# A graph network in one kernel: the middle stages in a written order, lin in operands 500 nodes wide, the edges' steps by twos

## The chip, the cores and the metric

The kernel runs on one core of a Trainium2 chip. The core has five engines that work at the same time and wait for each other through semaphores: TensorE (PE, with its weight loads as PEld), VectorE (DVE), ScalarE (ACT), GpSimd (POOL), and SyncE (SP), which issues most of the DMAs. The metric is the device time of one execution in microseconds (us); lower is better. All times below are in us unless marked otherwise.

## The reference

The input is x (1250 nodes x 1024), 20,000 directed edges with weights, and the parameters of two layers, each behind a layer norm and a ReLU, each added to its input. Cut to what matters:

```python
def layer0(x, src, dst, weight, wenc, benc, wdec, bdec, conv, lin):
    h = sigmoid(x @ wenc.T + benc)                   # 1250 x 500
    h2 = h @ conv
    agg = segment_sum(h2[src] * weight[:, None], dst)
    return (agg + h @ lin.T) @ wdec.T + bdec         # 1250 x 1024

def layer1(x, src, dst, W, b):                       # self loops added
    h = x @ W.T + b
    deg = count(row) + 1                             # row = src, or the node itself
    norm = deg[row] ** -0.5 * deg[col] ** -0.5
    return segment_sum(norm[:, None] * h[col], row)

h = relu(layernorm(x)); x = x + layer0(h, ...)
h = relu(layernorm(x)); x = x + layer1(h, ...)
```

## The kernel before

**Numbers in halves.** A float32 product is made of three matmuls on operands split into a high part (rounded for PE) and a low part (the rest): high x high, high x low, low x high. `product` (L342 to L352) issues them; its matmul stands at L347, so the encoder, lin, conv, the aggregation and the decoder all show that line, and are told apart by the tiles' names (penc, plin, pconv, pagg, pdec). A split costs a copy on ACT (high part) and a subtraction on DVE or POOL (low part).

**Stages.** Nodes are handled in 10 tiles of T = 125, or in NCH = 5 chunks of CH = 250. In the order of time:

- *Encoder* (`encode`): layer norm, transposition, x @ wenc.T and the sigmoid per chunk. It writes hT, the hidden values transposed (500 features as EC = 4 blocks of 125 rows, nodes as columns) in a high and a low part. Beside it the edges are read and turned into key columns for the one-hots.
- *lin* (`linear`): per chunk four products of 3 x 4 matmuls of 250 columns (plin). ACT copies each to hl.
- *conv* (`convolve`): per node tile one product of 12 matmuls of 500 columns (pconv), split into h2.
- *Aggregation* (`aggregate`): the edges become a dense matrix A (weights by source and destination), made while conv and the aggregation run. Per chunk four products of 3 x 10 matmuls of 250 columns (pagg). Each is closed by three operations: DVE adds it to hl (L702), ACT copies the high part (L703), DVE subtracts for the low part (L704). The results, agg, are the decoder's operands.
- *Decoder* (`decode`): per tile two halves of 12 matmuls of 512 columns (pdec), added to x by DVE; the sums go to DRAM through SP and are normed for the second layer.
- *Second layer*: products pz (L952) on counts of edges, the counts being loaded back transposed from DRAM (c_d to cr, L799), then pout (L1175), scaled by dinv, and the output.

**The edges' steps.** A step is PB = 5 groups of 5 destination nodes; there are 50. `one_hots` makes the operands of a step on DVE with three operations: L482 (640 elements per partition, which source residue), L486 (250, which block and destination), L490 (750, the same times the weight's three parts). `adjacency` takes a step that has been built: 15 small matmuls on PE (poh, 128 x 100 and 128 x 50), copies by ACT of the weights' high parts into A (L523, three pieces by APARTS) and of the counts (L529), and the low parts by DVE (L534, three pieces). After every fifth step a node tile's counts are whole: DVE adds the diagonal (L536), reduces the counts for the degrees (L537), and SP stores them to c_d (L538). `edge_work(n)`, called after each product or within it, adds n to an account, and while a whole step is owed, builds one and consumes one; two built steps stay ahead.

**Order of the work.** The encoder and everything from the decoder on stand in a written order (`tc.manual_schedule()`): each engine runs its instructions as the program has them. From lin to the decoder a planner reorders them (the context is left after the encoder and entered again before the decoder); it took 54 of lin's matmuls ahead of the encoder's last 8. Three pools of PSUM give the buffers: ps_acc with four accumulators for the products, ps_t with two, ps_oh with two for the steps' poh. Places in SBUF come from an arena whose offsets are a written list, PLAN, one for each allocation in order of the program; an instruction that writes a place waits for the last users of what lay there.

**Behind the aggregation.** `load` and `split` bring wdec in (four pieces, low parts on POOL at L632) after chunk 3's aggregation. The degrees' partial sums, degp, are summed by DVE, raised to the power -1/2 by POOL (dinv, L777), and stored by SP (L778). After this store in SP's order come the decoder's transposing loads of the counts (L799), the loads of x (L196) and the stores of the sums (x_d).

The calls of the stages, before:

```python
in_order.close()
for c in range(NCH):
    linear(c, lin, lambda: edge_work(0.8))
    if c == 1:
        cv = split_square("conv")
for c in range(NCH):
    convolve(c, cv, lambda: edge_work(1))
for c in range(NCH):
    aggregate(c, lambda: edge_work(0.8))
```

Of the kernel before, what the change touches and what calls it, by code (L numbers as in the profile page):

```python
# [35 lines left out]
P = 128  # L36
# [40 lines left out]
class Arena:  # L77
# [33 lines left out]
    6272, 1500, 3354, 1375, 0, 599, 1087, 3162, 3857, 346, 2032, 3729, 5890, 1750, 3479, 5390,  # L111
    4227, 4887, 2574, 4637, 5137, 5640, 2000, 3447, 1718, 1215, 5900, 6150, 2265, 567, 2824,
    3322, 4081, 535, 4509, 1718, 663, 2973, 1250, 2515, 0, 3857, 3953, 4951, 4919, 282, 32, 5140,
    1000, 1660, 1500, 398, 3223, 282, 494, 1718, 750, 526, 6118, 2015, 5890, 2829, 423, 5079,
    4111, 4008, 1250, 1500, 4638, 3399, 4606, 4866, 3777, 2831, 647, 5000, 3296, 5515, 5412,
    5309, 1853, 5103, 4263, 500, 4513, 3081, 4763, 3432, 2956, 5229, 3638, 4013, 3888, 5435,
    4866, 3329, 3081, 3535, 5332, 5140, 5060, 397, 4763, 0, 3535, 1750, 2000, 6297, 3208, 5265,
    5140, 103, 6015, 2162, 0, 5640, 2314, 3458, 250, 2497, 2417, 2721, 2064, 6297, 2618, 1147,
    147, 500, 750, 1016, 2337, 2721, 5037, 2456, 6265, 1141, 4410, 147, 44, 2314, 4660, 1141,
    1622, 2706, 3458, 4263, 3598, 1292, 6265, 5060, 3848, 5515, 147, 4638, 4079, 1542, 3862, 0,  # L120
    2328, 3348, 4182, 147, 3990, 5343, 4246, 4502, 3206, 5093, 0, 3598, 1672, 1280, 6178, 2956,
    5013, 6265, 5810, 5890, 6098, 5679, 4758, 5599, 2956, 2064, 5970, 4886, 5807, 4998, 6258,
    4758, 2496, 5679, 6112, 4838, 5952, 6240, 3428, 4758, 3348, 5639, 5879, 3990, 5839, 5599,
    5359, 5559, 2456, 5015, 4303, 5759, 4855, 5719, 5679, 5199, 6160, 5919, 6240, 3518, 6080,
    5519, 2888, 4695, 3348, 5359, 5759, 5039, 2888, 5519, 4879, 5199, 6240, 6200, 6160, 4695,
    3508, 5279, 5799, 5960, 5639, 3702, 5879, 6000, 3350, 5359, 3622, 3862, 5960, 5239, 6240,
    3478, 4695, 5079, 4855, 4951, 2916, 5519, 5639, 3734, 5799, 5159, 3606, 6000, 5279, 5385,
    1800, 6240, 1672, 1928, 2888, 5599, 5079, 4695, 5257, 5513, 3271, 4823, 2456, 5960, 2592,
    5671, 3143, 1280, 1536, 1408, 2135, 5921, 6022, 2928, 3007, 2513, 4445, 6150, 2849, 6229,
    4366, 2056, 6308, 5129, 5592, 2263, 2842, 6150, 4317, 5943, 5671, 2921, 2513, 6272, 2056,  # L130
    2592, 2135, 3064, 4445, 2842, 6022, 4616, 5592, 5079, 5943, 2263, 2056, 2985, 4303, 3064,
    5693, 6321, 4616, 2857, 5614, 2592, 2513, 4488,
# [4 lines left out]
def kernel(  # L137
# [35 lines left out]
    APARTS = ((0, 4), (4, 4), (8, 2))  # L173
# [301 lines left out]
    def one_hots(n):  # L475

        gs = slice(n * PB, (n + 1) * PB)
        eb, ek, ew = edges["eb"], edges["ek"], edges["ew"]
        t = arena.tile([P, PB * (P + 4 * M)], BF16, f"oh{n}")
        bo = t[:, : PB * P].rearrange("p (g b) -> p g b", g=PB)  # L480
        mv = t[:, PB * P :].rearrange("p (g q m) -> p g q m", g=PB, q=4)
        nc.vector.tensor_tensor(  # L482
            pairs(bo), pairs(cols).unsqueeze(1).to_broadcast([P, PB, P // 2, 2]),
            eb[:, gs].unsqueeze(2).to_broadcast([P, PB, P // 2, 2]), op=OP.is_equal,
        )
        nc.vector.tensor_tensor(  # L486
            pairs(mv[:, :, 0, :]), pairs(cols[:, :M]).unsqueeze(1).to_broadcast([P, PB, M // 2, 2]),
            ek[:, gs].unsqueeze(2).to_broadcast([P, PB, M // 2, 2]), op=OP.is_equal,
        )
        nc.vector.tensor_tensor(  # L490
            pairs(mv[:, :, 1:4, :]),
            pairs(mv[:, :, 0, :]).unsqueeze(2).to_broadcast([P, PB, 3, M // 2, 2]),
            ew[:, gs].unsqueeze(3).to_broadcast([P, PB, 3, M // 2, 2]), op=OP.mult,
        )
        built.append((n, bo, mv))

    def adjacency():
# [16 lines left out]
        arena.give(f"oh{n}")  # L514
# [20 lines left out]
        if k == per - 1:  # L535
            nc.vector.tensor_add(C[j][:T, j, :T], C[j][:T, j, :T], ident_b[:T, :T])  # L536
            nc.vector.tensor_reduce(degp[:, :, j], C[j][:T, :, :T], AX.X, OP.add)  # L537
            nc.sync.dma_start(c_d[j], C[j].rearrange("p a d -> p (a d)"))  # L538
            arena.give(f"cnt{j}")

    todo = list(range(NG // PB))
    owed = [0.0]

    def edge_work(n):

        owed[0] += n
        while owed[0] >= 1 - 1e-6 and (todo or built):
            owed[0] -= 1
            if todo:
                one_hots(todo.pop(0))  # L550
            if len(built) > 2 or not todo:
                adjacency()
# [13 lines left out]
    def encode(c, between):  # L566
        hi, lo = hn[c]
        hT[c] = arena.tile([T, 2, EC, CH], FR, f"hT{c}")
# [80 lines left out]
    def linear(c, lin, between):  # L649
        hl[c] = arena.tile([T, EC, CH], F32, f"hl{c}")  # L650
        for ec in range(EC):
            es = slice(ec * T, (ec + 1) * T)
            p = ps_acc.tile([P, 512], F32, tag="acc", name="plin")
            product(
                p[:T, :CH],
                [
                    ([lin(k, s)[:, es] for s in range(2)], [hT[c][:, s, k, :] for s in range(2)])
                    for k in range(EC)
                ],
            )  # L660
            nc.scalar.copy(hl[c][:, ec, :], p[:T, :CH])
            between()

    def convolve(c, cv, between):
        h2[c] = arena.tile([T, 2, 2, EMB], FR, f"h2_{c}")
        for i in range(2):
            p = ps_acc.tile([P, 512], F32, tag="acc", name="pconv")
            ns = slice(i * T, (i + 1) * T)
            product(
                p[:T, :EMB],  # L670
                [
                    ([hT[c][:, s, k, ns] for s in range(2)], [cv(k, s) for s in range(2)])
                    for k in range(EC)
                ],
            )
            nc.scalar.copy(h2[c][:, 0, i, :], p[:T, :EMB])
            nc.vector.tensor_sub(h2[c][:, 1, i, :], p[:T, :EMB], h2[c][:, 0, i, :])
            between()
        arena.give(f"hT{c}")
# [3 lines left out]
    def aggregate(c, between):  # L683
# [23 lines left out]
        arena.give(f"hl{c}")  # L707
# [36 lines left out]
    in_order.close()  # L744
# [3 lines left out]
    for c in range(NCH):  # L748
        linear(c, lin, lambda: edge_work(0.8))
        if c == 1:  # L750
            cv = split_square("conv")
    arena.give("lin0", "lin1")
    for c in range(NCH):
        convolve(c, cv, lambda: edge_work(1))
# [4 lines left out]
    wdec = []  # L759
    for c in range(NCH):  # L760
        aggregate(c, lambda: edge_work(0.8))
# [7 lines left out]
        elif c == 3:  # L769
            wdec.extend(split(f"wdec{k}", nc.gpsimd) for k in range(EC))  # L770
            load_x(1)
    arena.give(*(f"h2_{c}" for c in range(NCH)))
# [6 lines left out]

    in_order.enter_context(tc.manual_schedule())  # L780
# [853 lines left out]
```

## Time and profile before

| | |
|---|---|
| median of 3 runs | 487.01 (486.67 to 487.57) |
| the profiled execution | 487.37, its span 485.6 |
| TensorE's clock granted, mean | 0.993 of full speed |
| busy share of the span | PE 98%, PEld 89%, DVE 69%, ACT 36%, POOL 17% |
| lin | 76.8 to 112.8 |
| conv | 112.8 to 145.1 |
| aggregation | 145.1 to 230.8 |
| decoder | 230.8 to 286.4 |
| second layer, pz and pout | 286.4 to 480 |

The profile is one execution, recorded by the hardware; its span goes from the first recorded instruction to the last one's end, and 1.77 us of the execution's own time lie outside it. The page's first part gives each engine's busy time and its share of the span, with the number of instructions. A table by stage gives the same within chosen windows. The order in time of one engine lists start, length, engine, line, operation, tiles, shape, and, after an x, how many instructions in a row were merged into the row; the length of a merged row runs from the first start to the last end. Matmuls overlap in the pipeline, so a single length (0.28 at 250 columns) is longer than the distance between two starts. The chain that ended last runs through DVE from about 283.5 to 314.4, and from there through PE's pz and pout to the end.

### The profile page before, as it was taken

The numbers are of one execution on the slowest core, as the hardware profiler recorded it, in microseconds if no ns is written. First come the engines' busy times: TensorE is split into PE (matmuls) and PEld (weight loads), VectorE is DVE, ScalarE is ACT, GpSimd is POOL, SyncE is SP. The second block draws the span as 40 slices with busy tenths as digits, with TensorE's granted clock in tenths as the row PEclk, the third lists the DMA queues.
The fourth block names the chain that finished last, engine by engine and source line by source line (L and its number), as shares of the span: only waits on it lengthen the run. The fifth ranks groups of instructions, "written<-read, shape, count | busy, mean of one in ns | idle before, by whom it ended". The sixth has DMA issues, their size and how long they took to land. (4 is left out here: it accounts for less than half of the span.)

```text
span 485.6 us, 9225 instructions
## 1 busy us (share of the span) xinstructions
PE 474.9 (98%) x3614; PEld 431.2 (89%) x3614; DVE 336.0 (69%) x763; ACT 174.3 (36%) x453; POOL 81.5 (17%) x134
## 2 busy tenths in 40 slices
PE   6999999999999999999999999999999999999995
PEld 3999999998889999999878889999998887788784
DVE  6777479977697958884457776968798554555541
ACT  4585543553433243451253345323265021110000
POOL 4734252410000010161123641000000000000000
PEclk9899999999999999999999999999999999999998
DMA  8993103000000204401999621022429064445441
GB/s 284 368 272 85 32 2 84 1 29 28 29 29 28 70 4 135 164 1 29 205 253 262 200 86 45 2 82 92 163 79 236 11 165 112 112 122 128 124 97 49
DMA packets 50899, 52.20 MB, mean 108 GB/s; under 512 B 29728, under 2 KB 39592, under 8 KB 50847
## 3 DMA queue, kind: packets, MB, share of 16 engines
q1 hardware_dynamic: 50449, 51.09, 37.2%
q8 instruction: 30, 0.49, 0.4%
q0 software_dynamic: 320, 0.39, 0.3%
q14 instruction: 22, 0.18, 0.1%
q10 hardware_dynamic: 78, 0.05, 0.0%
HBM read 34.61 MB, written 17.45 MB: 107 GB/s over the span
## 5 line engine op out<-in xcount | busy, mean ns | idle before, releaser
L1175 PE MATMUL pout<-w,zs 128*125 128x512 f32 (+1 forms) x336 | 100.8, 383 | 0.0
L347 PE MATMUL pagg<-A,h 125*125 125x250 f32 x600 | 74.7, 282 | 0.0
L1175 PEld LDWEIGHTS pout<-w,zs 128*125 128x125 f32 x336 | 61.3, 186 | 14.1
L347 PEld LDWEIGHTS pagg<-A,h 125*125 125x125 f32 x600 | 71.4, 187 | 0.1
L347 PE MATMUL pdec<-wdec,agg 126*125 126x512 f32 x240 | 56.2, 395 | 0.0
L347 PEld LDWEIGHTS pdec<-wdec,agg 126*125 126x125 f32 x240 | 44.7, 187 | 11.1
L1183 DVE SCALAR_TENSOR_TENSOR res<-pout,dinv,res 125x512 f32<-125x512 f32 (+1 forms) x21 | 15.2, 725 | 49.5 <-PE pout L1175 49.5
L952 PE MATMUL pz<-cts,y 125*128 125x312 f32 (+1 forms) x320 | 47.3, 307 | 0.2 <-DVE cts L818 0.2
L952 PEld LDWEIGHTS pz<-cts,y 125*128 125x128 f32 x320 | 46.4, 189 | 0.5 <-DVE cts L818 0.5
L523 ACT CAST A<-poh 125x100 fp32r<-125x100 f32 x150 | 25.5, 258 | 49.3 <-PE poh L513 49.3
L534 DVE TENSOR_TENSOR A<-poh,A 125x100 fp32r<-125x100 f32 x150 | 26.9, 234 | 13.3 <-ACT cnt L529 12.8
L952 PE MATMUL pz<-ct,y 125*128 125x312 f32 (+1 forms) x240 | 35.7, 307 | 0.0
L952 PEld LDWEIGHTS pz<-ct,y 125*128 125x128 f32 x240 | 35.0, 189 | 0.1
L347 PE MATMUL penc<-hnh,wenc 128*125 128x250 f32 x256 | 34.3, 283 | 0.0
L482 DVE TENSOR_TENSOR oh<-cols,eb 128x640 bf16<-128x640 bf16 x50 | 25.9, 522 | 8.5 <-PE poh L513 6.2
L347 PEld LDWEIGHTS penc<-hnh,wenc 128*125 128x125 f32 x256 | 31.3, 187 | 0.0
L347 PE MATMUL plin<-hT,lin 125*125 125x250 f32 x240 | 30.1, 282 | 0.0
L347 PEld LDWEIGHTS plin<-hT,lin 125*125 125x125 f32 x240 | 28.6, 187 | 0.0
L347 PE MATMUL pconv<-conv,hT 125*125 125x500 f32 x120 | 28.6, 392 | 0.0
L508 PE MATMUL poh<-oh 128*128 128x100 bf16 x250 | 28.1, 206 | 0.0
L512 PE MATMUL poh<-oh 128*128 128x50 bf16 x250 | 27.1, 187 | 0.0
L513 PE MATMUL poh<-oh 128*128 128x50 bf16 x250 | 27.0, 184 | 0.0
(180 smaller groups left out, 843.4 us busy)
## 6 DMA issues: line engine op xcount, KB each, us to landing
x<-in_x_dram SPq DMA_DIRECT2D x14, 512.0 KB
x_d<-x SPq DMA_DIRECT2D x9, 512.0 KB
res<-x_d SPq DMA_DIRECT2D x9, 512.0 KB
out_dram<-res SPq DMA_DIRECT2D x19, 224.0 KB
c_d<-cnt SPq DMA_DIRECT2D x10, 320.0 KB
cr<-c_d SPq DMA_DIRECT2D x10, 312.5 KB
x<-in_x_dram SPq DMA_DIRECT2D x8, 256.0 KB
wencf<-in_wencT_dram SPq DMA_DIRECT2D x4, 500.0 KB
```

The lines of the kernel that those rows point to most:

```text
L347: nc.tensor.matmul(p, left[i], right[j], start=(part == 0 and n == 0), stop=(part == 2 and n == len(terms) - 1),)
L482: nc.vector.tensor_tensor(pairs(bo), pairs(cols).unsqueeze(1).to_broadcast([P, PB, P // 2, 2]), eb[:, gs].unsqueeze(2).to_broadcast([P, PB ...
L508: nc.tensor.matmul(p[:, g, :], left, mv[:, g, 0:2, :].rearrange("p q m -> p (q m)"), start=True, stop=False,)
L512: nc.tensor.matmul(p[:, g, M:], left, mv[:, g, 2, :], start=False, stop=False)
L513: nc.tensor.matmul(p[:, g, M:], left, mv[:, g, 3, :], start=False, stop=True)
L523: nc.scalar.copy(hi, whole)
L534: nc.vector.tensor_sub(lo, whole, hi)
L952: nc.tensor.matmul(p, left[m, which][:, s, j, :], right[:, j, c0:c1], start=(first and j == 0 and s == 0), stop=(last and j == NP - 1 and ...
L1175: nc.tensor.matmul(acc[u][:T, : cs.stop - cs.start], zs[t][:, i, half, m, :], w1[k][j][:, cs], start=(m == 0 and half == 0 and n == 0), st ...
L1183: nc.vector.scalar_tensor_tensor(x1[t][:, cs], acc[u][:T, : cs.stop - cs.start], dinv[:, t : t + 1], x1[t][:, cs], op0=OP.mult, op1=OP.add,)
```

## The change

Six things are edited.

- The written order is kept from the encoder's end to the decoder: `in_order.close()` and the later entry are removed. What was reordered by the planner now runs as the program has it.
- hT and hl are allocated for two chunks at once (the fifth alone), and `linear` handles such a pair: its products are 500 columns wide for the pairs and 250 for the last chunk. hT and hl are given back by pairs.
- `one_hots` builds two steps (OB = 10 groups) with each of its three operations. `edge_work` acts when two steps are owed: with six steps built, or none left to build, it first consumes two, then builds two. The amounts owed change: 0.8 for each chunk in lin's pairs, 1.2 in conv, 1 at each of the two calls in a product of the aggregation.
- A is one tile per chunk (APARTS of one piece), so L523 and L534 are one operation of 250 elements per step in place of three.
- The counts' diagonal is added by POOL. The degrees' reductions leave `adjacency`: `degrees` does them two at a time at the last ten calls of `beside` (the function called in the aggregation), and the rest, if any, after it. A count's buffer is given back there.
- conv's split stands after lin's first pair (before: after its second chunk), wdec's four splits at four of the same last calls (before: after chunk 3).

The list PLAN is new, as the allocations differ.

```diff
--- before.py
+++ after.py
@@ -108,28 +108,26 @@
 
 
 PLAN = (
...
 )
 
 
@@ -170,7 +168,8 @@
     NW = (E - WIN) // GRAN + 1
     NS = E // GRAN
     PB = 5
-    APARTS = ((0, 4), (4, 4), (8, 2))
+    APARTS = ((0, NT),)
+    OB = 2 * PB
 
     BASE = -(-nc.sbuf_base // 32) * 32
     ctx.enter_context(nc.sbuf_tensor("slab", [P, ARENA // 4], F32))
@@ -474,25 +473,27 @@
 
     def one_hots(n):
 
-        gs = slice(n * PB, (n + 1) * PB)
+        gs = slice(n * OB, (n + 1) * OB)
         eb, ek, ew = edges["eb"], edges["ek"], edges["ew"]
-        t = arena.tile([P, PB * (P + 4 * M)], BF16, f"oh{n}")
-        bo = t[:, : PB * P].rearrange("p (g b) -> p g b", g=PB)
-        mv = t[:, PB * P :].rearrange("p (g q m) -> p g q m", g=PB, q=4)
+        t = arena.tile([P, OB * (P + 4 * M)], BF16, f"oh{n}")
+        bo = t[:, : OB * P].rearrange("p (g b) -> p g b", g=OB)
+        mv = t[:, OB * P :].rearrange("p (g q m) -> p g q m", g=OB, q=4)
         nc.vector.tensor_tensor(
-            pairs(bo), pairs(cols).unsqueeze(1).to_broadcast([P, PB, P // 2, 2]),
-            eb[:, gs].unsqueeze(2).to_broadcast([P, PB, P // 2, 2]), op=OP.is_equal,
+            pairs(bo), pairs(cols).unsqueeze(1).to_broadcast([P, OB, P // 2, 2]),
+            eb[:, gs].unsqueeze(2).to_broadcast([P, OB, P // 2, 2]), op=OP.is_equal,
         )
         nc.vector.tensor_tensor(
-            pairs(mv[:, :, 0, :]), pairs(cols[:, :M]).unsqueeze(1).to_broadcast([P, PB, M // 2, 2]),
-            ek[:, gs].unsqueeze(2).to_broadcast([P, PB, M // 2, 2]), op=OP.is_equal,
+            pairs(mv[:, :, 0, :]), pairs(cols[:, :M]).unsqueeze(1).to_broadcast([P, OB, M // 2, 2]),
+            ek[:, gs].unsqueeze(2).to_broadcast([P, OB, M // 2, 2]), op=OP.is_equal,
         )
         nc.vector.tensor_tensor(
             pairs(mv[:, :, 1:4, :]),
-            pairs(mv[:, :, 0, :]).unsqueeze(2).to_broadcast([P, PB, 3, M // 2, 2]),
-            ew[:, gs].unsqueeze(3).to_broadcast([P, PB, 3, M // 2, 2]), op=OP.mult,
+            pairs(mv[:, :, 0, :]).unsqueeze(2).to_broadcast([P, OB, 3, M // 2, 2]),
+            ew[:, gs].unsqueeze(3).to_broadcast([P, OB, 3, M // 2, 2]), op=OP.mult,
         )
-        built.append((n, bo, mv))
+        for i in range(OB // PB):
+            of = slice(i * PB, (i + 1) * PB)
+            built.append((n * (OB // PB) + i, bo[:, of], mv[:, of]))
 
     def adjacency():
 
@@ -511,7 +512,8 @@
             )
             nc.tensor.matmul(p[:, g, M:], left, mv[:, g, 2, :], start=False, stop=False)
             nc.tensor.matmul(p[:, g, M:], left, mv[:, g, 3, :], start=False, stop=True)
-        arena.give(f"oh{n}")
+        if n % (OB // PB) == OB // PB - 1:
+            arena.give(f"oh{n // (OB // PB)}")
         v = p.rearrange("p g (w a d) -> p w a g d", w=2, d=GS)
         at = slice(i * PB * GS, (i + 1) * PB * GS)
         parts = [
@@ -533,23 +535,33 @@
         for whole, hi, lo in parts:
             nc.vector.tensor_sub(lo, whole, hi)
         if k == per - 1:
-            nc.vector.tensor_add(C[j][:T, j, :T], C[j][:T, j, :T], ident_b[:T, :T])
-            nc.vector.tensor_reduce(degp[:, :, j], C[j][:T, :, :T], AX.X, OP.add)
+            nc.gpsimd.tensor_add(C[j][:T, j, :T], C[j][:T, j, :T], ident_b[:T, :T])
             nc.sync.dma_start(c_d[j], C[j].rearrange("p a d -> p (a d)"))
-            arena.give(f"cnt{j}")
-
-    todo = list(range(NG // PB))
+            counted.append(j)
+
+    counted = []
+
+    def degrees(n):
+
+        for _ in range(n):
+            if counted:
+                j = counted.pop(0)
+                nc.vector.tensor_reduce(degp[:, :, j], C[j][:T, :, :T], AX.X, OP.add)
+                arena.give(f"cnt{j}")
+
+    todo = list(range(NG // OB))
     owed = [0.0]
 
     def edge_work(n):
 
         owed[0] += n
-        while owed[0] >= 1 - 1e-6 and (todo or built):
-            owed[0] -= 1
+        while owed[0] >= 2 - 1e-6 and (todo or built):
+            owed[0] -= 2
+            if len(built) >= 6 or not todo:
+                for _ in range(2):
+                    adjacency()
             if todo:
                 one_hots(todo.pop(0))
-            if len(built) > 2 or not todo:
-                adjacency()
 
 
     hT = {}
@@ -565,7 +577,12 @@
 
     def encode(c, between):
         hi, lo = hn[c]
-        hT[c] = arena.tile([T, 2, EC, CH], FR, f"hT{c}")
+        if c % 2 == 0:
+            wide = min(2, NCH - c) * CH
+            pair = arena.tile([T, 2, EC, wide], FR, f"hT{c}")
+            hT["pair", c] = pair
+            for i in range(wide // CH):
+                hT[c + i] = pair[:, :, :, i * CH : (i + 1) * CH]
 
         def left(k, ec, s):
             return wenc[k // 2][:, s, k % 2, ec * T : (ec + 1) * T]
@@ -647,18 +664,23 @@
     h2 = {}
 
     def linear(c, lin, between):
-        hl[c] = arena.tile([T, EC, CH], F32, f"hl{c}")
+
+        h = hT["pair", c]
+        wide = h.shape[3]
+        pair = arena.tile([T, EC, wide], F32, f"hl{c}")
+        for i in range(wide // CH):
+            hl[c + i] = pair[:, :, i * CH : (i + 1) * CH]
         for ec in range(EC):
             es = slice(ec * T, (ec + 1) * T)
             p = ps_acc.tile([P, 512], F32, tag="acc", name="plin")
             product(
-                p[:T, :CH],
+                p[:T, :wide],
                 [
-                    ([lin(k, s)[:, es] for s in range(2)], [hT[c][:, s, k, :] for s in range(2)])
+                    ([lin(k, s)[:, es] for s in range(2)], [h[:, s, k, :] for s in range(2)])
                     for k in range(EC)
                 ],
             )
-            nc.scalar.copy(hl[c][:, ec, :], p[:T, :CH])
+            nc.scalar.copy(pair[:, ec, :], p[:T, :wide])
             between()
 
     def convolve(c, cv, between):
@@ -676,7 +698,8 @@
             nc.scalar.copy(h2[c][:, 0, i, :], p[:T, :EMB])
             nc.vector.tensor_sub(h2[c][:, 1, i, :], p[:T, :EMB], h2[c][:, 0, i, :])
             between()
-        arena.give(f"hT{c}")
+        if c % 2 == 1 or c == NCH - 1:
+            arena.give(f"hT{c - c % 2}")
 
     aggT = {}
 
@@ -704,7 +727,8 @@
             nc.vector.tensor_sub(agg[:T, 1, ec], h, agg[:T, 0, ec])
             between()
         arena.give(*(f"A{c}_{i}" for i in range(len(APARTS))))
-        arena.give(f"hl{c}")
+        if c % 2 == 1 or c == NCH - 1:
+            arena.give(f"hl{c - c % 2}")
 
 
     parts = {}
@@ -741,24 +765,36 @@
         if c + 1 < NCH:
             begin_chunk(c + 1)
         encode(c, lambda n: between((c, n)))
-    in_order.close()
     cv = None
     lin = parts["lin"]
     arena.give(*(f"wenc{j}" for j in range(KD // 2)))
-    for c in range(NCH):
-        linear(c, lin, lambda: edge_work(0.8))
-        if c == 1:
+    for c in range(0, NCH, 2):
+        wide = hT["pair", c].shape[3] // CH
+        linear(c, lin, lambda: edge_work(0.8 * wide))
+        if c == 0:
             cv = split_square("conv")
     arena.give("lin0", "lin1")
     for c in range(NCH):
-        convolve(c, cv, lambda: edge_work(1))
+        convolve(c, cv, lambda: edge_work(1.2))
     arena.give("conv0", "conv1")
 
 
     wdec_v = wdecT.rearrange("(k p) e -> p k e", p=T)
     wdec = []
+
+    beside_left = [2 * EC * NCH]
+
+    def beside():
+        edge_work(1)
+        beside_left[0] -= 1
+        n = 2 * EC + 2 - beside_left[0]
+        if n > 0:
+            degrees(2)
+            if n <= EC:
+                wdec.append(split(f"wdec{n - 1}", nc.gpsimd))
+
     for c in range(NCH):
-        aggregate(c, lambda: edge_work(0.8))
+        aggregate(c, beside)
         if c == 1:
             load(T, wdec_v[:, 0, :], "wdec0", bdec)
             load(T, wdec_v[:, 1, :], "wdec1")
@@ -767,8 +803,8 @@
             load(T, wdec_v[:, 3, :], "wdec3")
             load_x(0)
         elif c == 3:
-            wdec.extend(split(f"wdec{k}", nc.gpsimd) for k in range(EC))
             load_x(1)
+    degrees(NT)
     arena.give(*(f"h2_{c}" for c in range(NCH)))
     arena.give("ed4")
     dinv = const.tile([T, NT], F32, name="dinv")
@@ -776,8 +812,6 @@
     nc.vector.tensor_reduce(deg, degp, AX.X, OP.add)
     nc.gpsimd.tensor_tensor(dinv, deg, half_neg[:T], op=OP.pow)
     nc.sync.dma_start(dinv_d.rearrange("(t p) -> p t", p=T), dinv)
-
-    in_order.enter_context(tc.manual_schedule())
```

## The prediction

> **What bounds the kernel now.** I read the page's busy shares first, then the engines' busy time by stage, then the order in time of TensorE (PE), of the DMA queue SP and of VectorE (DVE). Page and stages (columns of the second: window, its length, busy time and count for PE, PEld, DVE, ACT, POOL, then clock, DMA share, GB/s):
>
> ```profile
> PE 474.9 (98%) x3614; PEld 431.2 (89%) x3614; DVE 336.0 (69%) x763; ACT 174.3 (36%) x453; POOL 81.5 (17%) x134
> ...
> 76.80:112.80 36.00, 36.00 (x434) 35.56 (x433) 30.05 (x95) 17.70 (x71) 6.61 (x6) 1.00 0.15 47
> 112.80:145.10 32.30, 32.30 (x271) 26.51 (x270) 26.02 (x80) 12.04 (x49) 0.15 (x1) 1.00 0.06 22
> 145.10:213.90 68.80, 68.80 (x868) 68.05 (x867) 54.86 (x183) 28.77 (x131) 8.22 (x17) 1.00 0.21 71
> 213.90:230.80 16.90, 16.90 (x156) 16.86 (x156) 8.50 (x15) 3.46 (x10) 7.01 (x5) 1.00 0.10 21
> 230.80:286.40 55.60, 55.60 (x240) 44.50 (x240) 35.88 (x57) 21.38 (x27) 19.05 (x41) 1.00 0.85 215
> ```
>
> These are lin, conv, the aggregation with edges, its end, and the decoder. PE has no idle time in any of them, at full clock; no other engine is full. So what the change takes from DVE and ACT is worth nothing by itself: only PE's own work counts, and any new wait of PE. How closely PE is packed, from its order in time (start, length, merged matmuls):
>
> ```profile
> 97.03 3.49 PE L347 MATMUL plin<-hT,lin 125*125 125x250 f32 x28
> ...
> 101.35 5.26 PE L347 MATMUL plin<-hT,lin 125*125 125x250 f32 x43
> ...
> 118.06 5.89 PE L347 MATMUL pconv<-conv,hT 125*125 125x500 f32 x25
> ```
>
> A run lasts from its first start to its last end. Less the last matmul's own length (0.28 at 250 columns, 0.39 at 500) and the 0.08 us by which the first interval after a group of edge matmuls is longer (0.197 instead of 0.117 between single starts), the pitch is (5.26-0.28-0.08)/42 = 0.1167 us at 250 columns and (5.89-0.39-0.08)/24 = 0.2258 at 500.
>
> **The change, part by part.**
>
> *lin 500 wide.* 192 of the 240 matmuls of 250 columns become 96 of 500; the last chunk keeps 48. 192 x 0.1167 - 96 x 0.2258 = 22.41 - 21.68 = 0.73 us less, on PE's path. The Trainium skill, "TensorE: Matmul & The Clock Gate", section "Wait — 56ns, not 53.3ns?", has warm matmuls start N/2.4 GHz plus about 2.5 ns apart: 0.1067 and 0.2108, so 96 x 2.5 ns = 0.24 us saved. The rows lie above both figures (0.1167, 0.2258) and decide: 0.7, with 0.24 as the low end. ACT's copies become ten of 500 and four of 250 in place of twenty; nothing waits for them within a stage.
>
> *Edges by twos.* On PE the edge work is 50 steps of 15 matmuls. In the order of time they now stand in 31 groups, 12 of one step (0.50 us) and 19 of two (0.987). Each group costs 0.08 at the re-entry. By twos there are 25: six merges of two groups, each 2 x (0.50+0.08) - (0.987+0.08) = 0.09, together 0.56 us less, on the path.
>
> On DVE, single starts in a row give pitches of 0.20, 0.40 and 0.46 us for the one-hots' 250, 640 and 750 elements (L486, L482, L490): 0.07 + 0.52 ns per element. Two steps cost 2 x 1.06 = 2.12; ten groups at once 0.33+0.74+0.85 = 1.92. Splitting A's low part (L534) goes from three operations (0.46) to one of 250 (0.32, L702's pitch at that size). A pair of steps thus costs 2.56 on DVE. In the aggregation one pair falls to each product of 30 matmuls: PE 30 x 0.1167 + 1.07 = 4.57; DVE 2.56 + add, wait for ACT and subtract of agg (1.3) = 3.9. ACT: four copies of 250 (0.42, L529's row) and one of agg (0.40) = 2.1. The edge pair's PSUM banks come free when ACT has copied both parts and DVE has subtracted, some 1.4 and 2.2 us after the pair begins; the next pair comes 4.57 later. Three pairs of one-hots are ahead. No wait of PE: zero.
>
> *Counts' diagonal to POOL, conv and wdec splits beside it.* The add (L536, 0.216 on DVE) goes to POOL, for which I estimate 0.4 to 1 (its bf16 or fp32 operations of 125x256 take 0.46 to 0.73): ten times, off the path, only the store of the count waits. A rule of the Trainium skill speaks against this, in "SBUF — State Buffer", section "Who interferes with whom": DVE operations with two SBUF inputs and POOL operations that read SBUF exclude each other for the whole instruction, while a tensor_reduce never contends. The trace agrees (DVE's and POOL's order in time):
>
> ```profile
> 73.57 3.58 DVE L482 TENSOR_TENSOR oh<-cols,eb 128x640 bf16<-128x640 bf16 x4
> ...
> 73.26 2.33 POOL L632 TENSOR_TENSOR lin<-lin1f,lin 125x1000 fp32r<-125x1000 f32 x1
> ```
>
> The first of these four one-hots took 2.38 instead of 0.48. Where this bites after the change: conv's two splits, issued together after the first lin pair, are 2 x 2.34 of POOL (before: 3.69 at 85.9 and 2.34 at 95.8, ten us apart). Serialised with two sets of one-hots (1.92 each) that makes about 8.5 us of DVE, whereas PE meets three groups in the following 9 us. The last subtract ends about 0.3 us before PE wants its bank. Without the rule the margin would be some 3 us. I take zero, high end 0.7.
>
> *Degrees late.* Ten reductions (1.446, pitch 1.37) leave the middle and stand before the last products: two after the third product of chunk 3, four after its last, four after chunk 4's first. Call D the start of the decoder (230.86 now). DVE goes through 13.7 us of reductions from D-16.2 while four products' closings (1.3 each, five with the last) stand behind: the last subtract ends at about D+4.0. PE waits for closings only through its four accumulators: the decoder's first four products want theirs at D, D+2.8, D+5.6 and D+8.4; they are free at about D-6, D+0.4, D+1.7 and D+3.0. wdec's splits, issued by ACT from D-16 on, end on POOL at about D-2.4. No wait of PE.
>
> What is late is dinv: the sum over degp at D+4.2, POOL's power 2.0 (L777), so dinv's store at D+6.5. On SP the store stands before everything the decoder loads:
>
> ```profile
> 223.13 0.29 SPq L778 DMA_DIRECT2D dinv_d<-dinv  x1
> 230.58 4.77 SPq L799 DMA_TRANSPOSE cr<-c_d  x3
> 235.45 0.53 SPq L196 DMA_DIRECT2D x<-in_x_dram  x1
> 237.41 0.32 SPq L196 DMA_DIRECT2D x_d<-x  x1
> 237.78 6.84 SPq L799 DMA_TRANSPOSE cr<-c_d  x3
> 244.66 0.58 SPq L196 DMA_DIRECT2D x<-in_x_dram  x1
> ```
>
> Today the transposes start at D-0.3, after the change at about D+6.7: seven us later. SP had waited 1.4 before its store at 237.41, so x3's load is issued at about D+20 in place of D+13.8 and lands 4.2 later (its landing in the trace: 248.9), at D+24; DVE wants it at D+19.8. So DVE adds tile 3 four us late. PE needs that accumulator again four products on, at D+28; DVE is done by about D+25. SP's waits for DVE before each following store (2.4, 1.3, 2.2, 2.7 us) give the delay back by tile 5 or 6; the last tiles are used at their old places. Cost to PE: zero, with a margin of about 3 us. If the margin is gone, every us of delay is one of PE.
>
> *Order written down, new places in memory.* At the end of the encoder PE now takes lin's 54 early matmuls after the encoder's last 8; lin's low part was split at 75.6 and is wanted at about 80. Waits that follow from the new places (x8's load on chunk 0, conv's on chunks 2 and 3, x4's on tile 0's norm) are all for work ended before. Zero, plus or minus 0.3.
>
> *Sum.* 0.73 + 0.56 = 1.3 us less in a span of 485.6, whose own execution took 487.37 (1.77 lie around the span, unchanged); the three runs' median is 487.01, 0.36 under it. I take the sum off the median: 485.7.
>
> **Rivals.** (1) The gain comes at the low end (0.24 for lin, half of the merges), or small waits of 0.5 at the conv splits eat it: 486.2 to 487.5, inside what a measurement of this kernel tells from no change (0.2%, 0.97 us). For it: the gain is barely above that bound. Against: the pitches are steady over hundreds of matmuls. (2) Slower: dinv's store holds SP. It decides once x3's data land after about D+27, that is when the delay of the first transposes is over 10 us instead of 7: if closings behind the reductions collide with wdec's subtractions on POOL (2.4 each) and POOL's power is late as well, 12 us of delay are reached. Then PE waits 2 us at tile 5, and the tiles after it, which DVE meets late, pass part of it on into the chain of DVE operations that leads from 283.5 to 314.4 and leaves PE only 0.2 idle: 488 to 490. For it: DMA is 85% busy in that stage, so a late stream catches up poorly. Against: SP waited over 10 us for DVE there. (3) DVE becomes the bound in the aggregation: it would need over 4.57 per product against 3.9; at 5.0 it loses 13 x 0.4 = 5 us, less a lag of 3 that the banks allow: 488. The trace's pitches speak against it.
>
> **How the numbers follow.** The summed case has 0.48 (own range 484.9 to 486.0), the first rival 0.27, the second 0.17, the third 0.08. The range from 484.7 to 489.2 leaves out about one in ten at the top and little at the bottom, as there are no other us on PE to gain. Faster 0.48, same 0.27, slower 0.25.
>
> **What would show it.** lin: 96 matmuls of 500 columns at 0.226 apart and 48 of 250. The edge groups 25. No PE idle time between 77 and 286. The decoder's start near 229.5. dinv's store and the first transposes near D+6.5, DVE waiting for a DMA at tile 3, then at its old pace from tile 6. The one-hots' median near 0.80, 0.40 and 0.92 us. I am wrong if PE waits for DVE anywhere before 286, or if the chain at 283 to 314 grows.

## The result: 1.2% slower, where 0.3% faster was forecast

The changed kernel takes 493.1 us (median of 5 runs, 492.26 to 494.13), the kernel before 487.01; the ratio is 1.0122 (95% interval 1.0102 to 1.0142). The predicted 485.7 is 7.4 us off, and the time lies 3.9 us above the range. The profiled execution is the slowest of the five: 494.13, with a span of 492.2, which is 6.6 more than the 485.6 of before.

First the page's busy shares of the changed kernel, then its busy time by stage. The windows are cut at the same times as before (columns as there).

```profile
PE 476.2 (97%) x3518; PEld 426.7 (87%) x3518; DVE 325.4 (66%) x578; ACT 167.7 (34%) x345; POOL 84.6 (17%) x144
```

```profile
76.80:112.80 36.00, 34.82 (x333) 29.82 (x332) 24.76 (x38) 15.37 (x39) 6.62 (x6) 1.00 0.05 19
112.80:145.10 32.30, 32.30 (x273) 26.62 (x272) 22.18 (x38) 11.09 (x30) 1.02 (x4) 1.00 0.06 22
...
230.80:286.40 55.60, 51.57 (x216) 40.72 (x215) 33.87 (x57) 18.68 (x24) 18.19 (x39) 0.97 0.86 205
```

PE is no longer full everywhere: 1.18 us are missing in lin's window, 4.03 in the decoder's, and there the clock's mean has fallen to 0.97. VectorE and ScalarE have less work than before, as the change intended, and it buys nothing. PE's waits name the places (engine, line, what it waited for: us in total, times, longest):

```profile
PE pdec L346 <- DVE x L906: 4.0, 2, 3.3
...
PE poh L509 <- DVE A L536: 1.2, 1, 1.2
```

Neither wait is in the profile of before. To see what each stage lost or gained, I summed the distances between the starts of PE's matmuls by tile, each distance counted to the matmul it starts from:

| us | before | changed |
|---|---|---|
| lin (240 or 144 matmuls) | 28.63 | 29.22 |
| edge steps (750) | 24.83 | 24.65 |
| conv (120) | 27.61 | 27.60 |
| aggregation (600) | 71.67 | 71.41 |
| decoder (240) | 56.00 | 62.00 |

lin contains one stall of 1.35 (at 96.39, in front of an edge group); without it, it is 27.87, so 0.76 shorter. The decoder lost 6.0. The table holds 6.1 of the span's 6.6; nearly all of the rest, 0.5, lies behind the decoder.

**The decoder's queue.** SP's order in time in the changed kernel, whose decoder starts at D = 231.04 (columns: start, length, engine and line, kind, tiles):

```profile
237.05 0.28 SPq L814 DMA_DIRECT2D dinv_d<-dinv  x1
237.44 10.07 SPq L833 DMA_TRANSPOSE cr<-c_d  x3
247.62 0.52 SPq L195 DMA_DIRECT2D x<-in_x_dram  x1
248.19 0.42 SPq L195 DMA_DIRECT2D x_d<-x  x1
248.66 7.94 SPq L833 DMA_TRANSPOSE cr<-c_d  x3
256.64 0.58 SPq L195 DMA_DIRECT2D x<-in_x_dram  x1
```

dinv's store comes at D+6.0 and the transposes at D+6.4, where they were forecast (D+6.5 and D+6.7). But the first three take 10.07 us instead of the 4.77 of before. So x2's load is issued at D+16.6 and x3's at D+25.6, where the forecast had D+20 for x3's and passed over x2's (x2 and x3 are the input rows of node tiles 2 and 3). VectorE waits for both before its additions to these tiles, and PE waits for the accumulators that the additions free:

```profile
253.56 0.69 DVE L906 TENSOR_TENSOR x<-x,pdec 125x512 f32<-125x512 f32 x1 [9.47 <-PE pdec L346]
...
262.71 0.69 DVE L906 TENSOR_TENSOR x<-x,pdec 125x512 f32<-125x512 f32 x1 [6.17 <-DMA x<-in_x_dram]
```

```profile
254.31 5.87 PE L346 MATMUL pdec<-wdec,agg 126*125 126x512 f32 x24 [0.75 <-DVE x L906]
263.45 5.76 PE L346 MATMUL pdec<-wdec,agg 126*125 126x512 f32 x17 [3.27 <-DVE x L906]
```

The first row's label names PE, which had long been done; x2's load, issued at 247.62, is what came last (in the run with conv's splits on VectorE, below, the same addition is labelled with this load). PE is late by 0.92 at tile 4 and by 3.44 at tile 5 (distance between starts, less 0.233). Behind the second pause it runs slow: the first interval is 0.586, and six more are 0.427 in place of 0.233, until 266.6. The windows of that stretch, of the changed kernel and then of the kernel before, show the granted clock (third column from the right):

```profile
262.00:268.00 6.00, 4.55 (x13) 3.64 (x14) 5.16 (x9) 0.00 (x0) 2.08 (x5) 0.72 1.10 307
```

```profile
262.00:268.00 6.00, 6.00 (x28) 4.79 (x27) 4.52 (x8) 1.85 (x2) 1.97 (x4) 1.00 1.16 232
```

0.92 + 3.44 of waiting and 1.5 of slow starts make 5.9 of the 6.0. The half rate after a pause is what the Trainium skill describes in "TensorE: Matmul & The Clock Gate", section "What's actually happening"; section "Wait — 56ns, not 53.3ns?" gives 426.7 ns from start to start at 512 columns when cold, and the single starts here lie 426 to 427 ns apart. The first of these sections puts the half rate behind an idle window of about 3.4 us. That fits this pause of 3.44, but in the run with conv on VectorE (below) a pause of 2.43 was enough, so 3.4 is not the least that does it.

**The wait in lin.** VectorE's order in time in the changed kernel at the splits of conv, and POOL's:

```profile
90.49 0.90 DVE L536 TENSOR_TENSOR A<-poh,A 125x250 fp32r<-125x250 f32 x2 [6.68 <-ACT cnt L531]
91.30 0.82 DVE L481 TENSOR_TENSOR oh<-cols,eb 128x1280 bf16<-128x1280 bf16 x1
92.03 2.55 DVE L485 TENSOR_TENSOR oh<-cols,ed 128x500 bf16<-128x500 bf16 x1
94.62 2.96 DVE L489 TENSOR_TENSOR oh<-oh,ed 128x1500 bf16<-128x1500 bf16 x1
97.50 0.73 DVE L536 TENSOR_TENSOR A<-poh,A 125x250 fp32r<-125x250 f32 x2
...
98.89 0.41 DVE L485 TENSOR_TENSOR oh<-cols,ed 128x500 bf16<-128x500 bf16 x1
99.33 0.94 DVE L489 TENSOR_TENSOR oh<-oh,ed 128x1500 bf16<-128x1500 bf16 x1
```

```profile
91.93 2.38 POOL L649 TENSOR_TENSOR conv<-conv0f,conv 125x1000 fp32r<-125x1000 f32 x1 [16.28 <-ACT conv L648]
94.27 2.52 POOL L649 TENSOR_TENSOR conv<-conv1f,conv 125x1000 fp32r<-125x1000 f32 x1
```

Two one-hot operations (L485, L489) that take 0.41 and 0.94 elsewhere in this trace take 2.55 and 2.96 here and end 0.3 and 0.8 after POOL's two subtractions. The subtraction behind them, which frees the edge group's bank, starts at 97.50; PE had wanted that bank at 96.6. That POOL's subtractions are the cause is shown by the run that takes them away (conv's low parts on VectorE, below).

### The profile page after: what moved, and what is told of

Same layout as the page of the kernel before. It is cut to its first block, busy times and chain, and to the rows that moved or that the text cites. A ratio compares the mean times of both kernels' runs of the same rounds, so it can differ in the third digit from the quotient of the medians.

```text
span 492.2 us, 8731 instructions
## 1 busy us (share of the span) xinstructions
PE 476.2 (97%) x3518; PEld 426.7 (87%) x3518; DVE 325.4 (66%) x578; ACT 167.7 (34%) x345; POOL 84.6 (17%) x144
## 5 line engine op out<-in xcount | busy, mean ns | idle before, releaser
L346 PE MATMUL pagg<-A,h 125*125 125x250 f32 x600 | 73.6, 281 | 0.0
L346 PE MATMUL pdec<-wdec,agg 126*125 126x512 f32 x240 | 58.1, 404 | 4.0 <-DVE x L906 4.0
L346 PEld LDWEIGHTS pdec<-wdec,agg 126*125 126x125 f32 x240 | 45.7, 192 | 16.1 <-DVE x L906 4.9
L536 DVE TENSOR_TENSOR A<-poh,A 125x250 fp32r<-125x250 f32 x50 | 20.7, 416 | 20.8 <-ACT cnt L531 18.1
L346 PE MATMUL plin<-hT,lin 125*125 125x500 f32 (+1 forms) x144 | 29.0, 356 | 0.0
L509 PEld LDWEIGHTS <-oh 128*128 128x128 bf16 x250 | 23.8, 96 | 3.3 <-issue 2.6
L513 PE MATMUL poh<-oh 128*128 128x50 bf16 x250 | 26.6, 187 | 0.0
L514 PE MATMUL poh<-oh 128*128 128x50 bf16 x250 | 26.5, 184 | 0.0
L346 PEld LDWEIGHTS plin<-hT,lin 125*125 125x125 f32 x144 | 23.3, 186 | 3.6
L906 DVE TENSOR_TENSOR x<-x,pdec 125x512 f32<-125x512 f32 x20 | 13.5, 677 | 19.4 <-PE pdec L346 13.3
```

Of the source, the lines that this page charges most:

```text
L346: nc.tensor.matmul(p, left[i], right[j], start=(part == 0 and n == 0), stop=(part == 2 and n == len(terms) - 1),)
L509: nc.tensor.matmul(p[:, g, :], left, mv[:, g, 0:2, :].rearrange("p q m -> p (q m)"), start=True, stop=False,)
L513: nc.tensor.matmul(p[:, g, M:], left, mv[:, g, 2, :], start=False, stop=False)
L514: nc.tensor.matmul(p[:, g, M:], left, mv[:, g, 3, :], start=False, stop=True)
L536: nc.vector.tensor_sub(lo, whole, hi)
L906: nc.vector.tensor_add(xt[:, cs], xt[:, cs], p[:T, :])
```

## Experiments

Each edit stands alone on the changed kernel unless another base is named. Times are medians, and each ratio is to the kernel before on the same chip. The kernel before took 486.69 beside the runs "dinv's store behind the loads", "as late, but with fewer packets", "conv's low parts on VectorE" and "both edits together", 486.45 beside the last run, and 486.44 beside the other four.

**dinv's store behind the loads.**

```diff
-    nc.sync.dma_start(dinv_d.rearrange("(t p) -> p t", p=T), dinv)
...
+    steps[2 * NT - 1].append(
+        lambda: nc.sync.dma_start(dinv_d.rearrange("(t p) -> p t", p=T), dinv)
+    )
```

> The changed kernel, with one edit: the store of dinv stands on SP at the end of the decoder in place of ahead of its transposing loads; POOL's power is as late as in the changed kernel. Theory A (the store holds the queue, and x2's and x3's loads stand behind it): the first transposes start when the last reduction is done, at about D+0.1, take 4.8 us in place of 10.07, x2's load is issued near D+5, PE has no idle time in the decoder (its 240 intervals sum to 56.0 in place of 62.0), and the time falls by 6 from 493.1 to about 487.0. Rival B (VectorE's backlog of reductions and closings at the decoder's start makes it late, not the queue): the decoder stays at about 62 and the time at 493. Rival C (the transposes are slow by themselves after the change, from their new places): they start at D+0.1 but take 10; x2 is issued at D+10, PE still waits 0 to 2; 487 to 489.

Measured: 486.55, ratio 1.0004 (0.9994 to 1.0014). The first transposes start at 230.07 (D+0.1), where the last reduction lets them, and x2's load at D+4.9; the decoder's starts sum to 55.89, 0.1 less than before the change. VectorE's backlog of reductions and closings is as it was, and PE does not wait for it. Theory A holds; B and C are out.

```profile
230.07 4.62 SPq L832 DMA_TRANSPOSE cr<-c_d  x3
234.79 0.52 SPq L195 DMA_DIRECT2D x<-in_x_dram  x1
```

**The same late store in the kernel before.** This asks whether anything else of the change is needed for the loss.

```diff
@@ the kernel before, behind begin_counts("11", "21", "22") in place of ahead of it
+    for _ in range(3):
+        nc.gpsimd.tensor_tensor(dinv, deg, half_neg[:T], op=OP.pow)
+    nc.sync.dma_start(dinv_d.rearrange("(t p) -> p t", p=T), dinv)
```

> The kernel before, unchanged but for dinv: POOL's power stands behind the decoder's first memsets and is done three times (the same result), so that dinv's store, still ahead of the transposes on SP, comes at about D+6 as in the changed kernel, while the reductions, lin, the edges and the order stay as they were. Theory A (the late store with the slow transposes behind it is the whole loss): the first three transposes take 9 to 10 in place of 4.77, x2's load is issued near D+16, PE waits 4 to 6 in the decoder and the time is 491 to 493. Rival B (the loss needs VectorE's backlog or the new places too): 487 to 488.

Measured: 492.73, ratio 1.0118 (1.0098 to 1.0138), the loss of the change itself. The store came at D+6.2, the transposes took 10.94, the decoder's starts sum to 62.33, and PE waited at the same two tiles:

```profile
236.57 0.29 SPq L847 DMA_DIRECT2D dinv_d<-dinv  x1
236.95 10.94 SPq L797 DMA_TRANSPOSE cr<-c_d  x3
247.98 0.53 SPq L196 DMA_DIRECT2D x<-in_x_dram  x1
```

```profile
PE pdec L347 <- DVE x L873: 4.3, 2, 3.0
```

**As late, but with fewer packets.** dinv's store writes 1250 single numbers of 4 bytes, as the tile's columns lie across rows in DRAM. What is the size of the packets worth?

```diff
-    nc.sync.dma_start(dinv_d.rearrange("(t p) -> p t", p=T), dinv)
+    nc.sync.dma_start(dinv_d.rearrange("(p t) -> p t", p=T), dinv)
```

> The changed kernel, but dinv is stored as 125 packets of 40 bytes in place of 1250 of 4 bytes (the order of dinv in DRAM is then another, so the last stage scales by wrong factors; nothing else changes). It is as late as before, at D+6. Theory A1 (the many small packets slow the transposes that stand right behind them): the first three transposes take about 4.8 in place of 10.07, x2's load is issued near D+11.4 in place of D+16.6, and the decoder loses 0 to 1.5 in place of 6.1: 487 to 488.6. Rival A2 (the transposes are slow for another reason): 10 us still, 493.

Measured: 486.92, ratio 1.0008 (0.9998 to 1.0019). The store is at D+6.0 as in the changed kernel; the transposes take 5.28, and PE does not wait in the decoder (55.89):

```profile
235.46 0.28 SPq L814 DMA_DIRECT2D dinv_d<-dinv  x1
235.85 5.28 SPq L833 DMA_TRANSPOSE cr<-c_d  x3
241.24 0.52 SPq L195 DMA_DIRECT2D x<-in_x_dram  x1
```

```profile
255.35 0.69 DVE L906 TENSOR_TENSOR x<-x,pdec 125x512 f32<-125x512 f32 x1 [6.21 <-DMA x<-in_x_dram]
```

So the six us of lateness were hidden, as the prediction had it, though more narrowly: x3's load is issued at D+19.7 (forecast D+20), and VectorE is done with the addition that waits for it (the row above) at D+26.6 in place of the forecast D+25. PE wants that accumulator at D+28, so the margin was 1.4 and not 3. The five us that the small packets add were not hidden.

**conv's low parts on VectorE.**

```diff
-        ws = [split(f"{name}{j}", nc.gpsimd) for j in range(2)]
+        ws = [split(f"{name}{j}", nc.vector if name == "conv" else nc.gpsimd) for j in range(2)]
```

> The changed kernel, with the low parts of conv's two splits on VectorE in place of POOL. Theory A: POOL's two subtractions (2.3 each) stretch the one-hots beside them (L485 2.55 in place of 0.41, L489 2.96 in place of 0.94), so that the closing subtraction of the edge steps comes late and PE waits 1.35 at 96.4. With the splits on VectorE (about 1.1 each) the one-hots keep 0.41 and 0.94, the wait falls to 0 to 0.2 and the time by 1.2 to 1.35, to about 491.8. Rival B (VectorE is late by its own load: two splits on it are worse): the wait stays or grows, 493 to 494.

Measured: 490.42, ratio 1.0071 (1.0054 to 1.0089). lin's starts sum to 27.88 in place of 29.22 and PE no longer waits there: the two splits take 1.19 and 1.20 on VectorE, and the one-hots ahead of them 0.41 and 0.94.

```profile
91.85 0.41 DVE L485 TENSOR_TENSOR oh<-cols,ed 128x500 bf16<-128x500 bf16 x1
92.30 0.94 DVE L489 TENSOR_TENSOR oh<-oh,ed 128x1500 bf16<-128x1500 bf16 x1
93.15 1.19 DVE L649 TENSOR_TENSOR conv<-conv0f,conv 125x1000 fp32r<-125x1000 f32 x1
94.26 1.20 DVE L649 TENSOR_TENSOR conv<-conv1f,conv 125x1000 fp32r<-125x1000 f32 x1
...
PE pdec L346 <- DVE x L906: 2.3, 1, 2.3
```

The time fell by 2.7, twice what was expected. (PE's sums fell by 3.4, but the changed kernel's profiled execution is 1.0 above its median.) The rest is in the decoder, 59.98 in place of 62.00: the transposes took 9.28 there instead of 10.07, x2 was issued at D+15.8, and only the wait at tile 5 remains (2.43). What decides between 9.3, 10.1 and 10.9 for these transposes from one kernel to the next, the runs do not tell; so the 2.0 in the decoder is not shown to come from this edit.

**Both edits together** (store last, conv on VectorE).

> Both of these edits: the store of dinv at the decoder's end and conv's low parts on VectorE. Theory A: no wait of PE is left from lin to the decoder's end, so the sum of the prediction (1.3 less: 0.7 from lin, 0.6 from the edge groups) stands alone: 485.7, faster than before by 0.2 to 0.35%. Rival: the gain is not there (the stages up to the decoder are no shorter): 487.0.

Measured: 485.32, ratio 0.9973 (0.9964 to 0.9983), faster than both kernels. PE has no wait from lin to the decoder's end; in each of these windows (columns as before) its busy time equals the length:

```profile
76.50:110.30 33.80, 33.80 (x326) 29.04 (x326) 21.99 (x39) 15.29 (x39) 1.16 (x4) 1.00 0.05 20
110.30:142.80 32.50, 32.50 (x272) 26.56 (x271) 21.77 (x37) 11.10 (x30) 1.01 (x4) 1.00 0.06 21
142.80:228.10 85.30, 85.30 (x1022) 84.65 (x1021) 61.00 (x106) 27.85 (x78) 15.41 (x25) 1.00 0.18 61
228.10:284.00 55.90, 55.90 (x242) 44.76 (x241) 37.82 (x64) 22.18 (x29) 21.31 (x45) 1.00 0.80 217
```

Its sums are lin 27.88, edge steps 24.67, conv 27.60, aggregation 71.40, decoder 55.89: against before 0.75 + 0.16 + 0.01 + 0.27 + 0.11 = 1.30 less.

**lin 250 wide again in that kernel.**

```diff
+            for n0 in range(0, wide, CH):
+                p = ps_acc.tile([P, 512], F32, tag="acc", name="plin")
...
-                    ([lin(k, s)[:, es] for s in range(2)], [h[:, s, k, :] for s in range(2)])
+                        ([lin(k, s)[:, es] for s in range(2)], [h[:, s, k, n0 : n0 + CH] for s in range(2)])
...
-            nc.scalar.copy(pair[:, ec, :], p[:T, :wide])
+                nc.scalar.copy(pair[:, ec, n0 : n0 + CH], p[:T, :CH])
```

> The kernel with both edits, with lin's products 250 columns wide again (twice as many, the allocations kept). Theory A (the wide products give 0.73 of the 1.3): lin's stage 0.7 longer, 486.05 against 485.32. Rival (the width is worth only what the start of 96 matmuls costs, 0.24, or nothing): 485.3 to 485.6.

Measured: 486.28, ratio 0.9996 (0.9986 to 1.0005): the gain is gone. lin's starts sum to 28.46, 0.58 more than with the wide products. The medians say 1.0 (1.1 if each is set against the kernel before on its own chip), and the two intervals are each 1 us wide, so 0.58 from the trace is the better figure. By PE's sums this kernel should still be 0.7 under the kernel before, and the medians show 0.2; 0.7 is at the edge of the interval. The other 0.17 of lin's gain belongs to fewer edge groups within it, six in place of eight.

**The degrees early again**, with conv on VectorE (the store keeps its place).

```diff
+            nc.vector.tensor_reduce(degp[:, :, j], C[j][:T, :, :T], AX.X, OP.add)
             nc.sync.dma_start(c_d[j], C[j].rearrange("p a d -> p (a d)"))
-            counted.append(j)
+            arena.give(f"cnt{j}")
```

> The changed kernel with conv's splits on VectorE, and the degrees' reductions back in each fifth edge step. The store keeps its place ahead of the transposes, but dinv no longer waits for reductions: the sum over degp stands behind the last closing (D+1.3), the power ends at about D+3.5. Theory A (slow transposes whenever the 4-byte packets stand right ahead of them): the three transposes still take 9 to 10, from D+4, x2's load is issued near D+14, two us earlier than where PE began to lose; decoder 55.7 to 57, time 485.4 to 486.7. Rival: the transposes are fast again since the lateness itself made them slow: 4.8, x2 at D+9, 485.4. Rival: in the aggregation the reductions (1.4 each) delay the edges' closings and PE waits there.

Measured: 489.48, ratio 1.0055 (1.0037 to 1.0073), 2.8 above the top of the expected range. The queue did what theory A says: store at D+3.8, transposes 9.73 (slow even though two us earlier), x2 at D+14.0, and the decoder lost only 0.7. The last rival holds as well: in the aggregation PE waits three times for the edges' subtractions behind a reduction (0.45, 0.78 and 0.89). Its edge steps sum to 26.04 and its aggregation to 72.17, together 2.1 more than with the degrees late. So in this written order the late degrees do serve the aggregation.

```profile
235.92 0.28 SPq L815 DMA_DIRECT2D dinv_d<-dinv  x1
236.32 9.73 SPq L834 DMA_TRANSPOSE cr<-c_d  x3
...
PE poh L509 <- DVE A L536: 1.6, 3, 0.7
...
PE pdec L346 <- DVE x L907: 0.4, 1, 0.4
```

**The store from another queue**, with conv on VectorE.

```diff
-    nc.sync.dma_start(dinv_d.rearrange("(t p) -> p t", p=T), dinv)
+    nc.scalar.dma_start(dinv_d.rearrange("(t p) -> p t", p=T), dinv)
```

> The changed kernel with conv's splits on VectorE, and dinv's store issued by ScalarE's queue in place of SP's, at the same D+6. The first transposes then start at D+0.1 and are done (4.6) before the store; the second three run beside and behind it. Theory A1 (the small packets hold what follows on the same queue): the second three take 6 to 7 as in the run with the store last, no wait of PE, 485.4. Theory A2 (small packets slow any transfer of that time, in the memory or the DMA engines): the second three take 11 to 12, x3's load comes 5 later, at D+19.5, and is still in time: 485.4 to 486.5.

Measured: 485.13, ratio 0.9971 (0.9960 to 0.9982), as fast as both edits together. The first three transposes are through before dinv is ready (4.75). The second three, which then run beside and behind its packets, take 11.17, where they took 6.79 and 6.06 with the store last:

```profile
229.29 4.75 SPq L833 DMA_TRANSPOSE cr<-c_d  x3
...
236.07 11.17 SPq L833 DMA_TRANSPOSE cr<-c_d  x3
247.33 0.53 SPq L195 DMA_DIRECT2D x<-in_x_dram  x1
```

So it is not the place in SP's order: small packets from ACT's queue slow SP's transposes alike (A2). x3's load at D+18.2 is still in time.

**Small packets that stay in SBUF**, with conv on VectorE and the store last.

```diff
+    spare = const.tile([T, NT, 2], F32, name="spare")
+    nc.sync.dma_start(spare[:, :, 0], dinv)
```

> The changed kernel with conv's splits on VectorE; dinv's store to DRAM stands at the decoder's end, and in its old place, ahead of the transposes and as late, SP copies dinv within SBUF, again as 1250 packets of 4 bytes (into every second element of a spare tile). Theory M (it is the many small writes to DRAM that hold up the transposes' reads of DRAM): the first three transposes take 4.6 to 5.3, x2's load is issued near D+11.5, no wait of PE in the decoder, 485.4. Theory E (many small packets hold up whatever follows in the DMA engines, wherever they write): 9 to 10, x2's load near D+16, PE waits 4 in the decoder, 489 to 490.5.

Measured: 486.5 (485.36 to 489.87), ratio 0.9998 (0.9985 to 1.0011). The profiled execution is the slowest of twelve (489.87), but its queue is plain: the same number of 4-byte packets at the same place, and the transposes take 6.01.

```profile
235.89 0.94 SPq L815 DMA_DIRECT2D spare<-dinv  x1
236.94 6.01 SPq L834 DMA_TRANSPOSE cr<-c_d  x3
243.05 0.53 SPq L195 DMA_DIRECT2D x<-in_x_dram  x1
```

The traces also record each packet. The 1250 packets of 4 bytes run from 237.9 to 239.4 in the changed kernel and from 237.5 to 239 here. Behind them the transposes' packets of 256 bytes go at 500 to 940 per us here (before the change, 680 to 870). In the changed kernel they go at 80 to 260 per us from 240 to 246, and only then at over 900. So theory M is much the nearer: small writes to DRAM hold up the reads of DRAM behind them, for six us after the last of them was sent. It is not the whole: within SBUF, too, the packets cost the transposes 1.2 to 1.5, and the median is 1.1 above the 485.4 expected. In the profiled execution x2's load is issued at D+13.2 and x3's at D+22.1, and PE waits 1.2 for tile 3's accumulator, which fits the narrow margin found above; for a second stop of 1.85, among the pz, the profile shows no cause.

The Trainium skill has a line that bears on this ("DMA: Bandwidth & Descriptors", "Specifications"): below 512 bytes the DMA engine reads, modifies and writes. But the packets of 40 bytes and those within SBUF are below 512 bytes too and cost little, so the line alone does not explain the delay. Shown is that it needs DRAM as the target and the many packets; what it is that takes the time there stays open, and also whether it matters that all 1250 fall into the same 5 KB of DRAM.

## Why the prediction was wrong, by its steps

*lin 500 wide* was right in kind and a little high: 0.73 was forecast for the width, and it is worth 0.58 (6 ns for each of the 96 matmuls saved). lin is 0.75 shorter; the rest is fewer edge groups in it. The pitch of the trace came nearer than the page's 2.5 ns per matmul (0.24). The prediction's own rows show the weight loads (PEld) busy for 35.56 of lin's 36.00, so its "no other engine is full" does not hold there; whether they set the pitch at 250 columns was not tested.

*Edges by twos* was right on PE (25 groups; 0.56 forecast). By the sums, lin's 0.17, the edge steps' 0.16 and the aggregation's 0.27 make 0.60. VectorE and ScalarE never bounded the aggregation; the third rival is out.

*The sum* of 1.3 was right in size: 1.30 in PE's starts and 1.37 in the medians, once the two waits are gone. That it fits to the digit is luck: the two forecast parts give 0.58 + 0.60 = 1.18, and 0.12 came from conv and the decoder, of which nothing was expected.

*conv's splits beside it* was mis-sized: "I take zero, high end 0.7", measured 1.35. The rule of mutual exclusion, weighed there, did bite: one set of one-hots and POOL's two subtractions together took 6.3 (91.3 to 97.6); the 4.7 and 1.92 of the prediction's working add up to 6.6. What failed was the time that PE leaves: "PE meets three groups in the following 9 us", with the last subtraction done 0.3 before its bank is wanted. A wide product of 12 starts and a group follow each other in 3.8, so the third group came 7.6 after the first (89.0 to 96.6) and wanted the second's bank, which came free 1.35 later.

*Degrees late* is the step that failed: "Cost to PE: zero, with a margin of about 3 us", measured 6.0. Its times up to the store were right within half a us. The reductions, which the prediction took as free of POOL, were that: four beside wdec's subtractions on POOL took 5.54, 1.38 each. Two things were not right. It took the first transposes to need what they needed before (4.8), and they took 10.07 because a store of 1250 small packets now stood directly ahead; in the trace of before the same store came 7.5 us ahead of them and was over. And it followed only x3: x2's load, issued straight behind those transposes, was late first. The second rival had the place (SP, x3, "PE waits 2 us at tile 5") and the amount of delay at which it decides (over 10; x3's load was 11.8 later relative to D). But it named closings and POOL as what would stretch seven us to twelve, and these were on time; and its 488 to 490 stopped short. The prediction also left out the clock, which turned 4.4 us of waiting into 5.9.

*Order written down* cost nothing that the sums show: conv is unchanged, and no wait but those at the conv splits and in the decoder appears.

## What to carry to other kernels

When a step moves a DMA, ask what stands behind it in the memory and not only behind it in its queue: this one was 5 KB and 0.3 us long in SP's row, and cost five us to the transfers after it, from either of the two queues tried. A store of single numbers belongs where nothing waits for DRAM for a while, or in longer pieces (40 bytes were enough here). And a pause of PE costs more than its length: count the slow matmuls behind it.

## What the runs showed of the hardware that was not expected

- 1250 packets of 4 bytes to DRAM made three transposing loads behind them take 9.3 to 10.9 us in place of 4.5 to 4.8. As 125 packets of 40 bytes they cost 0.5 to 0.7, and as 4-byte packets within SBUF 1.2 to 1.5, about what the packets themselves take.
- A pause of PE of 2.43 us was enough for some 3 us at half the rate (six starts 0.427 apart, in the run with conv on VectorE); pauses of 1.35 and 0.92 were not.
- POOL's fp32 subtraction of 125 x 1000 elements took 2.4, and two of them stretched the one-hots beside them on VectorE by 2.1 and 2.0. The same subtraction took 1.2 on VectorE, so giving it to POOL cost VectorE more time (4.2) than doing it (2.4).
